# Two heads' short softmax rows in one buffer, turned by one transpose, in a causal attention and feed-forward kernel

## The chip, the cores and the metric

The kernel runs on one core of a Trainium2 chip, in fp32. The metric is device time in microseconds (us) of one execution. A core has five engines that run side by side, each in its own instruction order: TensorE (PE, matrix multiplies; PEld is its weight load), VectorE (DVE), ScalarE (ACT), GpSimd (POOL) and SyncE (SP, which here issues the DMA transfers). PE writes into PSUM banks; the other data lie in SBUF, 128 partitions wide.

## The reference

```python
# x: (8, 1024, 256); 16 heads of 64
def attn(x):                                    # Wq, Wk, Wv: (16, 256, 64); Wp: (1024, 256)
    idx = clip(pos[None, :] - pos[:, None] + 16, 0, 32)
    bias = transpose(rel_table[idx], (2, 0, 1))
    q, k, v = (einsum('btc,hcd->bhtd', x, W) for W in (Wq, Wk, Wv))
    scores = einsum('bhtd,bhsd->bhts', q, k) / sqrt(64) + bias[None]
    w = softmax(where(causal, scores, -inf), axis=-1)
    out = einsum('bhts,bhsd->bhtd', w, v)
    return out.transpose(0, 2, 1, 3).reshape(8, 1024, 1024) @ Wp + bp
def ffn(x):
    x_prev = x shifted by one row of T (zeros first)
    xr, xk = mu * x + (1 - mu) * x_prev         # with mu_r and mu_k
    return sigmoid(xr @ W_r.T) * (square(relu(xk @ W_k.T)) @ W_v.T)
x = x + layernorm(attn(layernorm(x)))
x = x + layernorm(ffn(layernorm(x)))
```

## The kernel before

The attention is cut into 64 units: 8 batch rows times 8 pairs of heads. The 1024 query rows of a unit are 8 blocks (`tb` 0 to 7) of 128 rows. Block `tb` needs scores against the first n = 128 (tb + 1) keys only. Blocks 4 to 7 are "long" (n over 512, done in two parts), blocks 0 to 3 are "short". A unit has four steps, each with one long and one short block (`STEPS`).

For one block, `do_scores` records these tasks. PE multiplies q and k of both heads into PSUM (line 1041; 64-row tiles, so that two heads and two halves of the rows run together; short blocks take two of the four shared `pm` banks, long blocks their own ring `sl`). DVE adds the bias near the diagonal (line 1070) and takes the negated row maximum (line 1078). ACT writes the exponentials from PSUM to an SBUF buffer `p` of one head and sums them (line 1098), which frees the bank. DVE takes the reciprocal of the sum (line 1165). POOL scales `p` in place (line 1186), one instruction for a short block of one head, two for a long one.

`turn` then has DVE transpose `p` in 32 x 32 blocks into the tile `blocks` (line 1207), one instruction for each head. `blocks` has the axes `[partition, r, slot, head, 32]`; a slot is a 32-column block of one row block. When the row blocks of a group (`GROUPS`: two groups of four row blocks in each unit) are turned, `shuffle` issues 16 DMA copies from SP (line 1267) that move 32-partition bands from `blocks` to a tile `d`, so that the blocks become full transposes. `do_av` multiplies `d` with v on PE (line 1293), and ACT saves the result (line 1316). In the last unit the second group, tb 4, 2, 5 and 3, is transposed by PE instead (`turn_by_pe`). All other matmuls (projections, the feed-forward part) go through the helper at line 433 with 128-row tiles.

Buffers come from rings: a `Ring` of n buffers gives the next owner its buffer when the users of the owner n places before are done. The ring for short `p` has four buffers of 512 columns, the one for long `p` four of 1024. In the last batch row the feed-forward part borrows such rings for its tiles (`buf` in `stages_ffn`).

The order of the work is not that of the source. `add` records a task with its engine, a guessed cost and its dependencies. `Planner.simulate` plays all tasks with these costs; each engine takes, of the tasks that are ready, the one with the lowest key, and the instructions are issued in that order. A key is the task's own priority plus `RANK` of its kind (named after its functions, so `dve:one.go` is the transpose of one head), times 9. The plan is cut into stretches of 34 us; for each, a seed in `SEEDS` draws random offsets for the ranks of all kinds, in the order of their sorted names (seed 0: none), and for the planner's reluctance to let PE pass between score tiles (64 rows) and the other matmuls (128 rows), for which it reckons 0.09 us. A prologue (the first loads and projections) is planned before, without seeds.

Of the kernel before, what the change touches and what calls it, by code (L numbers as in the profile page):

```python
# [92 lines left out]

STRETCH = 34
SEEDS = (
    392905, 816692, 244547, 283470, 560662, 39100, 216772, 294259, 588279, 412218,
    371534, 0, 431774, 883409, 180062, 984965, 373709, 0, 0, 0,
    763639, 658110, 822178, 930278, 665013, 718545, 0, 952361, 100832, 846644,
    0, 137572, 647438, 377597, 0, 469262, 83528, 641677, 323164, 611824,
    444950, 813510, 452093, 622742, 919130, 335621, 0, 751616, 573689, 0,  # L100
    0, 99909, 466380, 402426, 0, 986219, 146830, 82811, 0, 0,
    151578, 369797, 955240, 0, 0,
)


# [252 lines left out]
def tile_attn_ffn_block(  # L358
# [16 lines left out]
    nc = tc.nc  # L375
    B, T, C = x.shape
    H, _, D = Wq.shape
    P = 128
    NT = T // P
    NC = C // P  # L380
# [4 lines left out]
    CT = 2 * P  # L385
    HB = 512
    BW = P + MAX_REL
    WL = P - 1 + BW
    QD = 32
    NQ = P // QD  # L390
# [25 lines left out]
    acts = ctx.enter_context(tc.tile_pool(name="acts", bufs=1))  # L416
# [3 lines left out]
    add = plan.add  # L420
# [8 lines left out]
    def matmul(dst, lhs, rhs, first, last):  # L429
# [21 lines left out]
        "v": Ring(acts, [P, NT, P], "v", 1),  # L451
        "sl": Ring(ps_l, [P, 2, HB], "sl", 2),
        ("p", "long"): Ring(acts, [P, T], "pl", 4),
        ("p", "short"): Ring(acts, [P, HB], "ph", 4),
        "carry": Ring(small, [P, NC], "carry", 2),
    }
    for what in ("in", "ao", "y", "f"):
# [294 lines left out]
    def stages_ffn(b, c):  # L752

        box = {}

        def buf(name, tag, spare):

            if b < B - 1:
                return R[tag](f"{name}_{b}_{c}")
            return R[spare](  # L760
                f"{name}_{b}_{c}", lambda t: t[:, : NC * CT].rearrange("p (k f) -> p k f", k=NC)
            )

        def s0(prio):
            box["rn"] = norm_stats(ys[b, c], f"y_{b}_{c}", prio)

        def s1(prio):
            box["yn"] = buf("yn", "yn", ("p", "short")) if c % 2 else R["yn"](f"yn_{b}_{c}")
            normed(box["yn"], ys[b, c], box["rn"], f"y_{b}_{c}", prio, edge=b == B - 1)

        def s2(prio):
# [175 lines left out]
    NU = len(units)  # L947
# [67 lines left out]
    def do_scores(u, tb, prio):  # L1015


        n = (tb + 1) * P
        size = "long" if n > HB else "short"
        parts = [(0, n // 2), (n // 2, n)] if n > HB else [(0, n)]  # L1020
        pr = units[u][1]
        q, k = qkv[u, "q"], qkv[u, "k"]
        what = f"{u}_{tb}"
        ps = [R["p", size](f"p_{what}_{hh}") for hh in range(2)]
        nmax, tot, rcp = (R[x, size](f"{x}_{what}") for x in ("nmax", "tot", "rcp"))
        z = {"u": u, "tb": tb, "n": n, "p": ps}

        def part(i, c0, c1):

            sl = R["sl"](f"s_{what}_{i}") if size == "long" else None  # L1030
            keep = [sl] if sl else []

            def s(hh):
                return sl.tile[:, hh, : c1 - c0] if sl else pm(t, hh)[:, : c1 - c0]

            def go():
                for half in range(2):
                    for hh in range(2):
                        rows = slice(hh * D, (hh + 1) * D)
                        o = half * D  # L1040
                        nc.tensor.matmul(  # L1041
                            s(hh)[o : o + D],
                            q.tile[rows, tb * P + o : tb * P + o + D],
                            k.tile[rows, c0:c1],
                            start=True,
                            stop=True,
                        )

            t = add(
                "pe",  # L1050
                0.05 + (c1 - c0) * 0.00169,
                go,
                r=[(q, tb // 4)] + [(k, g) for g in range((c1 - 1) // HB + 1)],
                w=keep,
                prio=prio,
                mode="rows",
                banks=0 if sl else 2,
            )
            z.setdefault("scores", t)
            w = min(n, BW)  # L1060
            ready = {hh: t for hh in range(2)}

            def bias(h0, h1):
                def go():
                    if sl:
                        dst = sl.tile[:, :, c1 - c0 - w : c1 - c0]
                        src = bm[:, 2 * pr : 2 * pr + 2, BW - w :]
                    else:
                        dst, src = s(h0)[:, n - w : n], bm[:, 2 * pr + h0, BW - w :]
                    nc.vector.tensor_tensor(dst, dst, src, ALU.add)  # L1070

                cost = 0.07 + (h1 - h0) * w / 960
                done = add("dve", cost, go, t, bm_done, r=keep, prio=prio - 0.5)
                ready.update({hh: done for hh in range(h0, h1)})

            def top(h0, h1):
                def go():
                    nc.vector.tensor_reduce(  # L1078
                        nmax.tile[:, i, h0:h1],
                        sl.tile[:, :, : c1 - c0] if sl else s(h0),  # L1080
                        AX.X,
                        ALU.max,
                        negate=True,
                    )

                return add(
                    "dve",
                    0.075 + (h1 - h0) * (c1 - c0) / 960,
                    go,
                    ready[h0],  # L1090
                    r=keep,
                    w=[(nmax, i)],
                    prio=prio - 0.5,
                )

            def exp(hh, max_done):
                def go():
                    nc.scalar.activation(  # L1098
                        ps[hh].tile[:, c0:c1],
                        s(hh),  # L1100
                        AF.Exp,
                        bias=nmax.tile[:, i, hh : hh + 1],
                        scale=1.0,
                        accum_out=tot.tile[:, i, hh : hh + 1],
                    )

                add(
                    "act",
                    0.26 + (c1 - c0) * 0.00083,
                    go,  # L1110
                    max_done,
                    r=keep,
                    w=[ps[hh], tot],
                    prio=prio - 0.1,
                    frees=None if sl else (t, hh),
                )

            if sl:
                if c1 == n:
                    bias(0, 2)  # L1120
                done = top(0, 2)
                for hh in range(2):
                    exp(hh, done)
            else:
                for hh in range(2):
                    bias(hh, hh + 1)
                    exp(hh, top(hh, hh + 1))
# [7 lines left out]
        if size == "long":  # L1135
            total = R["part", size](f"part_{what}")

            def behind():
# [10 lines left out]
                r=[rcp],  # L1149
                w=[rcp],  # L1150
                prio=prio - 0.1,
# [14 lines left out]
            r=[total],  # L1166
            w=[inv],
            prio=prio - 0.6,
        )
        if size == "long":  # L1170
# [6 lines left out]
                r=[inv, rcp],  # L1177
                w=[rcp],
# [3 lines left out]
        def scale(hh):  # L1182
            def go():
                for i, (c0, c1) in enumerate(parts):
                    p = ps[hh].tile[:, c0:c1]
                    nc.gpsimd.tensor_scalar(  # L1186
                        p, p, rcp.tile[:, i, hh : hh + 1], 1.0, ALU.mult, ALU.mult
                    )

            cost = 0.25 * len(parts) + n / 1220  # L1190
            add("pool", cost, go, r=[ps[hh], rcp], w=[ps[hh]], prio=prio)

        for hh in range(2):
            scale(hh)
# [2 lines left out]
    def turn(z, prio):  # L1197

        tb, n, u = z["tb"], z["n"], z["u"]
        k = tb // 2  # L1200
        g = 0 if k in GROUPS[0] else 1
        s0 = GROUPS[g][k] + 1 - tb % 2
        state = blk.setdefault(g, {"turns": [], "move": []})

        def one(hh, p):
            def go():
                nc.vector.transpose(  # L1207
                    blocks[g][:, :, s0 : s0 + 2 * tb + 1 : 2, hh, :].rearrange(
                        "p r a j -> p a r j"
                    ),  # L1210
                    p.tile[:, :n].rearrange("p (a r j) -> p a r j", r=NQ, j=QD),
                )

            state["turns"].append(
                add("dve", 0.065 + n / 960, go, *state["move"], r=[p], prio=prio)
            )

        for hh in range(2):
            one(hh, z["p"][hh])

    def turn_by_pe(z, g, prio):

        tb, u = z["tb"], z["u"]
        s0 = GROUPS[g][tb // 2] + 1 - tb % 2
        if (u, g) not in dd:
            dd[u, g] = R["d"](f"d_{u}_{g}")
# [2 lines left out]
        def some(hh, a0, a1):  # L1229
            def go():  # L1230
                for a in range(a0, a1):
                    matmul(
                        pm(t)[:, (a - a0) * P : (a - a0 + 1) * P],
                        z["p"][hh].tile[:, a * P : (a + 1) * P],
                        ident,
                        True,
                        True,
                    )

            t = add("pe", 0.217 * (a1 - a0), go, r=[z["p"][hh]], prio=prio, banks=1)  # L1240

            def place():
                n = a1 - a0
# [311 lines left out]
```

## Time and profile before

| | |
|---|---|
| median of 3 runs | 2194.66 us (2192.37 to 3990.92) |
| profiled execution, its own time | 2193.71 us |
| its span in the profile | 2191.9 us |
| granted TensorE clock, mean | 0.998 |
| busy PE, PEld | 2161.1 us (99%), 1182.6 us (54%) |
| busy DVE, ACT, POOL | 1970.5 us (90%), 1377.4 us (63%), 1526.8 us (70%) |
| transposes at line 1207 | 1016, 724.2 us |
| POOL scales at line 1186 | 1536, 883.9 us |

An engine's busy time is the time in which it has an instruction at work. Rows of groups read "line, engine, operation, output <- inputs, shapes, count | total busy us, mean ns of one | idle us of the engine just before them, and what ended it". In PE's timeline a row merges equal matmuls that follow each other; one fp32 matmul of the source leaves two records there, so `x8` of 512 columns is four matmuls. Ends of matmuls are modelled and overlap the next start; starts are not. A row of stretches gives the stretch, its length, then busy time and count for PE, PEld, DVE, ACT and POOL, the granted PE clock, the DMA engines' busy share and GB/s.

### The profile page before, as it was taken

To read this page: it belongs to the slowest core of one execution; us is meant where nothing else is said; L and a number is where in the kernel's file an instruction comes from. 1 tells how busy PE (TensorE), PEld (TensorE's weight loads), DVE (VectorE), ACT (ScalarE), POOL (GpSimd) and SP (SyncE) were. 2 spreads that over 40 slices of the span, in tenths; PEclk is the share of its full clock that TensorE was granted. 3 is DMA by queue.
4 is the path that set the end of the run, shared out by engine and by line. 5 is a ranking of instruction groups with operands and counts; after the bars stand their busy time and mean duration, and the time that the engine had idled before them with its cause. 6 is when DMAs were issued, how large, how long until landed. Compare 5 with 4: busy or idle time off the path is not lost.

```text
span 2191.9 us, 61295 instructions
## 1 busy us (share of the span) xinstructions
PE 2161.1 (99%) x21312; PEld 1182.6 (54%) x21312; DVE 1970.5 (90%) x4460; ACT 1377.4 (63%) x4314; POOL 1526.8 (70%) x3709
## 2 busy tenths in 40 slices
PE   7999999999999999999999999999999999999997
PEld 3455555555555555555555555555555555555565
DVE  5998999999998999998999989899889998999776
ACT  5665756666566565665656666565666756667454
POOL 4666677766786768775687766777667775687553
PEclk9999999999999999999999999999999999999999
DMA  5887877867778687776877777777787868877560
GB/s 166 193 199 184 194 175 179 202 167 181 178 179 200 166 193 177 183 189 169 196 180 188 181 189 181 170 175 192 170 190 178 198 167 198 193 177 189 131 152 25
DMA packets 272596, 388.92 MB, mean 177 GB/s; under 512 B 142624, under 2 KB 199968, under 8 KB 272160
## 3 DMA queue, kind: packets, MB, share of 16 engines
q1 hardware_dynamic: 272144, 384.87, 73.3%
q8 instruction: 170, 2.79, 0.6%
q14 instruction: 138, 1.13, 0.2%
q10 hardware_dynamic: 144, 0.14, 0.0%
HBM read 59.91 MB, written 25.29 MB: 39 GB/s over the span
## 4 chain that ended last, share of the span: by engine, by line
PE 89%; DVE 5%; DMA 1%; POOL 1%; issue 1%; ACT 1%; SPq 1%; ACTq 0%; DVEq 0%; POOLq 0%
PE pm L433 46%; PE pm L1293 21%; PE s L1041 16%; PE pm L1041 6%; DVE blocks L1207 2%; DVE nmax L1078 2%; POOL p L1186 1%; SPq L1267 1%; ACT p L1098 0%; DMA d<-blocks 0%; DVE pm L1070 0%; DMA out_dram<-r 0%; DVE s L1070 0%; DMA tab<-in_L_attn_rel_table_dram 0%; DVE y L722 0%
## 5 line engine op out<-in xcount | busy, mean ns | idle before, releaser
L1186 POOL TENSOR_SCALAR p<-p,rcp 128x512 f32<-128x512 f32 (+5 forms) x1536 | 883.9, 595 | 86.0 <-DVE rcp L1165 62.7
L1098 ACT ACTIVATE p<-s,nmax 128x512 f32<-128x512 f32 (+3 forms) x1024 | 616.0, 607 | 398.4 <-DVE nmax L1078 317.4
L1207 DVE STREAM_TRANSPOSE blocks<-p 128x256 f32<-128x256 f32 (+2 forms) x1016 | 724.2, 749 | 50.6 <-POOL p L1186 41.6
L1078 DVE TENSOR_REDUCE nmax<-s 128x2 f32<-128x1024 f32 (+3 forms) x512 | 516.7, 1009 | 33.3 <-PE s L1041 30.1
L1293 PE MATMUL pm<-d,v 128*64 128x256 f32 (+1 forms) x5120 | 523.5, 359 | 0.3 <-DMA d<-blocks 0.3
L1293 PEld LDWEIGHTS pm<-d,v 128*64 128x64 f32 x5120 | 351.8, 137 | 219.4 <-issue 39.6
L1041 PE MATMUL s<-k,q 64*64 64x512 f32 (+3 forms) x4096 | 444.3, 519 | 5.9 <-ACT p L1098 5.7
L1098 ACT ACTIVATE p<-pm,nmax 128x256 f32<-128x256 f32 (+3 forms) x512 | 270.9, 531 | 94.5 <-DVE nmax L1078 68.9
L433 PEld LDWEIGHTS pm<-wv,xnT 128*64 128x64 f32 x4096 | 226.5, 137 | 52.0 <-issue 26.9
L433 PE MATMUL pm<-wv,xnT 128*64 128x128 f32 x4096 | 248.1, 274 | 0.0
L433 PE MATMUL pm<-xnT,wk 128*64 128x512 f32 x1024 | 245.5, 600 | 0.1
L1078 DVE TENSOR_REDUCE nmax<-pm 128x1 f32<-128x256 f32 (+3 forms) x512 | 242.1, 478 | 3.4
L433 PE MATMUL pm<-xnT,wq 128*64 128x512 f32 x1024 | 244.7, 599 | 0.0
L433 PE MATMUL pm<-wp_sb,oT 128*64 128x256 f32 x2048 | 240.5, 381 | 0.7 <-ACT oT L1316 0.7
L1041 PEld LDWEIGHTS s<-k,q 64*64 64x64 f32 x4096 | 133.6, 132 | 180.2 <-issue 95.2
L1098 ACT ACTIVATION_READ_ACCUMULATOR p<-s,nmax 128x1 f32 x1024 | 206.7, 202 | 0.0
L433 PEld LDWEIGHTS pm<-wp_sb,oT 128*64 128x64 f32 x2048 | 141.6, 137 | 101.7 <-issue 25.2
L1041 PE MATMUL pm<-k,q 64*64 64x256 f32 (+3 forms) x2048 | 188.4, 438 | 0.0
L1070 DVE TENSOR_TENSOR pm<-pm,bm 128x144 f32<-128x144 f32 (+1 forms) x512 | 135.3, 298 | 38.1 <-PE pm L1041 36.9
L1140 POOL TENSOR_TENSOR rcp<-nmax 128x2 f32<-128x2 f32 x256 | 51.0, 199 | 148.5 <-DVE nmax L1078 119.0
L1155 POOL TENSOR_TENSOR tot<-tot,rcp 128x4 f32<-128x4 f32 x256 | 52.1, 203 | 146.8 <-ACT rcp L1148 139.8
L433 PEld LDWEIGHTS pm<-xnT,wq 128*64 128x64 f32 x1024 | 68.0, 137 | 129.7 <-issue 104.4
(103 smaller groups left out, 2266.2 us busy)
## 6 DMA issues: line engine op xcount, KB each, us to landing
d<-blocks SPq DMA_DIRECT2D x2032, 144.0 KB, 2.6
xin<-in_L_attn_x_dram SPq DMA_DIRECT2D x32, 256.0 KB, 3.0
wq<-in_L_attn_Wq_dram SPq DMA_DIRECT2D x128, 64.0 KB, 2.2
wk<-in_L_attn_Wk_dram SPq DMA_DIRECT2D x128, 64.0 KB, 2.2
wv<-in_L_attn_Wv_dram SPq DMA_DIRECT2D x64, 128.0 KB, 2.9
xre<-in_L_attn_x_dram SPq DMA_DIRECT2D x32, 256.0 KB, 3.0
out_dram<-r SPq DMA_DIRECT2D x32, 256.0 KB, 2.2
via_in<-st_in SPq DMA_DIRECT2D x112, 64.0 KB, 1.9
```

The costliest lines, as they stand in the source:

```text
L433: nc.tensor.matmul(dst[rows], lhs[:, rows], rhs, start=first, stop=last)
L1041: nc.tensor.matmul(s(hh)[o : o + D], q.tile[rows, tb * P + o : tb * P + o + D], k.tile[rows, c0:c1], start=True, stop=True,)
L1070: nc.vector.tensor_tensor(dst, dst, src, ALU.add)
L1078: nc.vector.tensor_reduce(nmax.tile[:, i, h0:h1], sl.tile[:, :, : c1 - c0] if sl else s(h0), AX.X, ALU.max, negate=True,)
L1098: nc.scalar.activation(ps[hh].tile[:, c0:c1], s(hh), AF.Exp, bias=nmax.tile[:, i, hh : hh + 1], scale=1.0, accum_out=tot.tile[:, i, hh : h ...
L1140: nc.gpsimd.tensor_tensor(rcp.tile[:, 0, :], m1, m0, ALU.subtract)
L1155: nc.gpsimd.tensor_tensor(tot.tile, tot.tile, rcp.tile, ALU.mult)
L1186: nc.gpsimd.tensor_scalar(p, p, rcp.tile[:, i, hh : hh + 1], 1.0, ALU.mult, ALU.mult)
L1207: nc.vector.transpose(blocks[g][:, :, s0 : s0 + 2 * tb + 1 : 2, hh, :].rearrange("p r a j -> p a r j"), p.tile[:, :n].rearrange("p (a r j) ...
L1267: nc.sync.dma_start(d.tile[r * QD : (r + 1) * QD, q].rearrange("p s h j -> p (s h j)"), blocks[g][q * QD : (q + 1) * QD, r].rearrange("p s ...
L1293: nc.tensor.matmul(dst, v[:, jt, rows], src, start=(jt == 0), stop=(jt == 2 * k + 1),)
```

## The change

For short blocks, both heads' exponentials now go into one buffer of 1024 columns. They lie in turn by blocks of 32 columns: 32 of head 0, 32 of head 1, and so on. `p_of` gives the view of one head, which ACT writes and POOL scales. One DVE transpose (`both` in `turn`) then reads the 2n columns and writes both heads' slots, whose 32 columns lie side by side in `blocks`. In the last unit, tb 2 and 3 go to `turn_by_pe`; there the heads lie one after the other. The ring for short `p` becomes two buffers of 1024 columns. In the last batch row the feed-forward tile `yn` of c = 1 moves to the ring of v and that of c = 3 to the ring of long `p`. `dve:both.go` has no entry in `RANK` (the transpose of one head, `dve:one.go`, has 1.8). All 65 seeds are replaced. The built program has 254 DVE instructions fewer; PE, ACT, POOL and SP have as many as before, in another order.

```diff
 SEEDS = (
-    392905, 816692, 244547, 283470, 560662, 39100, 216772, 294259, 588279, 412218,
...
+    424466, 663855, 192028, 0, 417825, 336004, 961170, 927691, 447616, 808813,
...
-        ("p", "short"): Ring(acts, [P, HB], "ph", 4),
+        ("p", "short"): Ring(acts, [P, 2 * HB], "ph", 2),
...
-            box["yn"] = buf("yn", "yn", ("p", "short")) if c % 2 else R["yn"](f"yn_{b}_{c}")
+            box["yn"] = buf("yn", "yn", "v" if c == 1 else ("p", "long")) if c % 2 else R["yn"](f"yn_{b}_{c}")
...
-        ps = [R["p", size](f"p_{what}_{hh}") for hh in range(2)]
+        if size == "long":
+            ps = [R["p", size](f"p_{what}_{hh}") for hh in range(2)]
+        else:
+            ps = [R["p", size](f"p_{what}")] * 2
+        mixed = size == "short" and (u < NU - 1 or tb < 2)
...
+        def p_of(hh, c0, c1):
+            if size == "long":
+                return ps[hh].tile[:, c0:c1]
+            if not mixed:
+                return ps[hh].tile[:, hh * n : (hh + 1) * n]
+            return ps[hh].tile[:, : 2 * n].rearrange("p (b h j) -> p b h j", h=2, j=QD)[:, :, hh, :]
...
                     nc.scalar.activation(
-                        ps[hh].tile[:, c0:c1],
-                        s(hh),
+                        p_of(hh, c0, c1),
+                        same(s(hh)),
                         AF.Exp,
...
-                    w=[ps[hh], tot],
+                    w=[(ps[hh], hh), tot],
...
-                    p = ps[hh].tile[:, c0:c1]
+                    p = p_of(hh, c0, c1)
                     nc.gpsimd.tensor_scalar(
...
-            add("pool", cost, go, r=[ps[hh], rcp], w=[ps[hh]], prio=prio)
+            add("pool", cost, go, r=[(ps[hh], hh), rcp], w=[(ps[hh], hh)], prio=prio)
...
+        def both(p):
+            def go():
+                nc.vector.transpose(
+                    blocks[g][:, :, s0 : s0 + 2 * tb + 1 : 2, :, :].rearrange(
+                        "p r a h j -> p a r (h j)"
+                    ),
+                    p.tile[:, : 2 * n].rearrange("p (a r j) -> p a r j", r=NQ, j=2 * QD),
+                )
+
+            state["turns"].append(
+                add("dve", 0.065 + 2 * n / 960, go, *state["move"], r=[p], prio=prio)
+            )
...
+        if z["p"][0] is z["p"][1]:
+            return both(z["p"][0])
         for hh in range(2):
             one(hh, z["p"][hh])
```

## The prediction

> **What bounds the kernel now.** I read the page first, for engine shares and the chain; then the stretches of the span; then PE's timeline, start to start; then the groups by shape for prices; last, the waits and the landing of the shuffles.
>
> ```profile
> PE 2161.1 (99%) x21312; PEld 1182.6 (54%) x21312; DVE 1970.5 (90%) x4460; ACT 1377.4 (63%) x4314; POOL 1526.8 (70%) x3709
> PE 89%; DVE 5%; DMA 1%; POOL 1%; issue 1%; ACT 1%; SPq 1%; ACTq 0%; DVEq 0%; POOLq 0%
> ```
>
> PE is busy 99% of the 2191.9 us and holds 89% of the chain that ended last; DVE comes second. The stretches (length, then busy time of PE, PEld, DVE, ACT, POOL) show where PE is not fed:
>
> ```profile
> 0.00:100.00 100.00, 86.22 (x778) 41.64 (x778) 72.77 (x165) 62.74 (x185) 54.19 (x143) 0.98 0.69 179
> ...
> 500.00:1000.00 500.00, 499.98 (x4934) 272.85 (x4932) 460.37 (x1048) 320.22 (x1010) 365.99 (x882) 1.00 0.77 183
> 1000.00:1500.00 500.00, 498.07 (x4901) 270.82 (x4898) 463.31 (x1042) 321.19 (x1017) 363.51 (x881) 1.00 0.76 181
> 1500.00:2140.00 640.00, 639.99 (x6404) 356.13 (x6402) 568.78 (x1275) 396.44 (x1248) 443.13 (x1078) 1.00 0.74 177
> 2140.00:2192.00 52.00, 39.25 (x412) 27.28 (x408) 35.86 (x115) 25.29 (x51) 19.23 (x38) 0.93 0.08 26
> ```
>
> Only the first 100 us and the last 52 us have holes. Since busy PE is not PE at its peak, I went to PE's timeline and took starts of successive groups:
>
> ```profile
> 2069.46 0.66 PE L1041 MATMUL pm<-k,q 64*64 64x256 f32 x8
> 2069.95 1.90 PE L1041 MATMUL s<-k,q 64*64 64x512 f32 x16
> 2071.77 1.95 PE L433 MATMUL pm<-wp_sb,oT 128*64 128x256 f32 x16
> 2073.55 1.89 PE L433 MATMUL pm<-xnT,wk 128*64 128x512 f32 x8
> 2075.27 1.92 PE L433 MATMUL pm<-wv,xnT 128*64 128x128 f32 x32
> 2077.11 0.45 PE L1041 MATMUL pm<-k,q 64*64 64x128 f32 x8
> ```
>
> The eight 512-column records at 2073.55 are followed 1.72 us later. The closest such pair (108.13 and 109.84 us) is 1.71 apart. I set the price at 1.707 us for 4096 columns on the 128-row array (two records at a time) and for 8192 columns of the 64-row score matmuls (four at a time); what is too little in it shows up in the borders below. By that price all matmuls need 2037.8 us. What exceeds it lies at borders between groups. From 100 to 2140 us the medians are 0.056 us from score group to score group (380 borders), 0.015 us from 128-row group to 128-row group (768), but 0.110 us into scores (272) and 0.115 us out of them (273): 2075.27 to 2077.11 is 1.84, not 1.72. The whole span is 8.4 before the first matmul + 2037.8 + 136.2 at borders + 9.5 after the last matmul. Of the 136.2, only 24.4 us lie in gaps over 0.35 us, which are true stalls: 12.3 before 100 us, 6.3 (eight places) from 100 to 2140 us, 5.8 after. So even a kernel without one stall would take 2167.5 us, 1.1% less.
>
> **The change, part by part.**
>
> *Transposes.* For each row block tb of 0 to 3, two DVE transposes become one of twice the width. Both sizes have rows:
>
> ```profile
> L1207 DVE STREAM_TRANSPOSE blocks<-p 128x1024 f32<-128x1024 f32 x128 | 153.8, 1219 | 6.4 <-POOL p L1186 5.7
> ...
> L1207 DVE STREAM_TRANSPOSE blocks<-p 128x768 f32<-128x768 f32 x126 | 116.0, 944 | 5.5 <-POOL p L1186 4.4 <-DMA via_in<-st_in 0.7
> ...
> L1207 DVE STREAM_TRANSPOSE blocks<-p 128x512 f32<-128x512 f32 x126 | 83.0, 686 | 7.4 <-POOL p L1186 5.6 <-DMA d<-blocks 1.1 <-DMA wk<-in_L_attn_Wk_dram 0.2
> ...
> L1207 DVE STREAM_TRANSPOSE blocks<-p 128x384 f32<-128x384 f32 x126 | 66.4, 552 | 7.1 <-POOL p L1186 7.1
> ...
> L1207 DVE STREAM_TRANSPOSE blocks<-p 128x256 f32<-128x256 f32 x128 | 50.4, 422 | 10.4 <-POOL p L1186 5.2 <-DMA d<-blocks 3.4 <-POOL part L1156 1.1
> ...
> L1207 DVE STREAM_TRANSPOSE blocks<-p 128x128 f32<-128x128 f32 x128 | 31.8, 281 | 2.2 <-POOL p L1186 2.1
> ```
>
> Saved per pair: 2 x 281 - 422 = 140 ns, 2 x 422 - 686 = 158, 2 x 552 - 944 = 160, 2 x 686 - 1219 = 153. Times 64, 64, 63 and 63 pairs (the last unit turns tb 2 and 3 on PE): 9.0 + 10.1 + 10.1 + 9.6 = 38.8 us of DVE in 254 instructions fewer. DVE goes to about 1932 us (88%). None of it is on the path in the steady part: DVE's 10% idle is already there and PE's holes there sum to 6.3 us. Those eight holes stand mostly behind ACT's exponentials, which wait for DVE's maxima; I book -2 us, bounds 0 and -6.3.
>
> *The wait that is added.* A merged transpose waits for both heads' POOL scales, so the pair lands later by the merged duration less one short one: 141, 264, 392, 533 ns, 333 on average. Behind it on DVE stand the next bias adds and maxima, for which ACT's exponentials wait. What follows the transposes are SP's 16 shuffle copies (L1267, issued over about 10 us, landing 2.6 us later), then the value matmuls at L1293. From the last landing to the first such matmul the median slack is 12.2 us over 127 shuffles, the 10% point 4.0, the 5% point 2.0, the least 0.46. A delay of 0.53 us is late in one or two cases: 0 to 1 us, taken as 0.5. Without that cover it would be 127 x 0.53 = 67 us. SP's own copies are the same in number.
>
> *Buffers.* Four buffers of 512 columns become two of 1024: still two row blocks deep. In the tail, xr moves onto this ring of two, and yn of c = 1 and 3 onto v and the long ring. The built order shows the third xr behind the PE group that reads the first, ten PE groups ahead of its own use: hidden, 0.
>
> *Exponentials and scales in runs of 32 columns.* ACT has a row in 32-column runs: the 256-column oT copy takes 377 ns, and two ordinary 512-column rows, 590 ns for v and 600 for q, with the 0.83 ns a column between the exponentials of 320 and 512 columns (528 to 687), come down to 377 to 388 at 256. So 0 for ACT. POOL has no row with runs. Its 512 short scales take 46.4 + 62.5 + 128 x 0.601 + 128 x 0.700 = 275 us now. Lower bound 0 (ACT's case); upper bound 83% more, as the slowest 512-column POOL row (1281 ns at L571) stands to 700 ns: +228 us, POOL at 80%, each scale 0.45 us later. Even then POOL is not the bound, but shuffles with under 2 us of slack (6 of 127) and some exponentials come late: about +10 us at most. I take 0, the scale being, like ACT's copy, one stream in and one out, where the L571 row reads two. [...]
>
> *New seeds.* They redraw the order of all work after the prologue. In the built order PE crosses between score and 128-row groups 610 times, 570 before: 20 more each way. Each pair replaces one border of 0.056 and one of 0.015 by 0.110 + 0.115: 20 x 0.154 = +3.1 us (40 full borders would be 4.5). This is on the path, since PE has no slack. [...]
>
> **Sum.** The profiled execution took 2193.7 us (span 2191.9 and 1.8 around it). 2193.7 + 3.1 (crossings) - 2 (stalls) + 0.5 (later landings) = 2195.3; the shown median lies 1 us above the profiled time. I forecast 2195 us: no change. About 2% is what a measurement of this kernel can tell from no change. Own range: down by the other 4.3 us of steady stalls and the 4.9 us of stalls between 60 and 100 us, to about 2184; up by 1.4 (full crossings), POOL's 10 and the start's stalls drawn once more (4.9), to about 2212.
>
> **Rivals.**
>
> *A relieved DVE feeds PE everywhere* (5%). All stalls after 60 us go, tail included: 2193.7 - 4.9 - 6.3 - 5.8 + 3.1 = 2180. For it: exponentials wait 386 us for maxima. Against: those waits do not reach PE now. Even this is only 0.6% faster; over 2% (under 2150.8) would need matmul work to vanish, and not one matmul is removed, so 1% for that.
>
> *The short ring stalls PE* (5%). A merged transpose frees both heads' buffer 0.333 us later on average; the new kind of task also has no entry in the planner's rank list, where the single transpose had 1.8. If the next short exponential then waits, it keeps two of the four pm banks and PE stands. All 256 pairs at 0.333 us: 85 us, 2193.7 + 85 + 3 = 2282. It decides the verdict from 41 us on (2238 is 2%), that is 124 pairs passing their wait to PE. For it: banks and ring are shared and POOL's order changes. Against: exponentials wait for these transposes three times now, 3.2 us in all.
>
> *It does not do what it says* (3%): runs of 64 columns slow the merged transpose until it costs its two halves. DVE keeps 1970 us, and 2193.7 + 3.1 + 0.5 = 2197 follows.
>
> The forecast itself has 86%; the last 1% is over 2% faster. The rivals at 2180 and 2197 and all of the forecast lie within 2%; the ring rival is shared, four of its five parts above 2% and one below; mishaps of the new order add a little to the slow side: faster 0.01, same 0.94, slower 0.05.
>
> **What would show it.** Right: one merged row per width at 422, 686, 944 and 1219 ns, DVE near 1932 us, PE still 98 to 99%, 610 crossings at 0.11 us, scales in runs at 375 to 700 ns. Wrong: new waits of PE on p or on ACT's exponentials, of ACT on the transposes, scale rows far over 700 ns, or more than 20 us of PE gaps over 0.35 us between 100 and 2140 us.

## The result, and the profile after

The changed kernel takes 2199.82 us (median of 11 runs, 2198.43 to 2201.55), the kernel before 2193.29 us (11 runs, one of them far off at 3990.92 us, the others 2191.45 to 2195.83). The ratio is 1.0031, 95% interval 1.0023 to 1.004: 6.5 us slower, within the 2% and inside the stated range, but clear of noise, and 5 us above the forecast. The profiled execution took 2199.11 us, its span is 2197.3 us, 5.4 us longer than before.

The page of the changed kernel, shares of the engines and the chain that ended last:

```profile
PE 2166.3 (99%) x21312; PEld 1179.6 (54%) x21312; DVE 1955.4 (89%) x4206; ACT 1382.0 (63%) x4314; POOL 1518.2 (69%) x3709
...
PE 93%; DVE 3%; DMA 1%; SPq 1%; ACT 1%; POOL 0%; issue 0%; ACTq 0%; POOLq 0%; DVEq 0%
```

DVE lost its 254 instructions and 15.1 us. PE has the same 21312 records but is busy 5.2 us longer, and holds still more of the chain. The same stretches as before (length, then busy PE, PEld, DVE, ACT, POOL):

```profile
0.00:100.00 100.00, 85.77 (x772) 40.98 (x774) 75.06 (x160) 63.31 (x187) 56.18 (x147) 0.98 0.68 177
...
500.00:1000.00 500.00, 497.59 (x4868) 268.77 (x4868) 453.67 (x976) 316.39 (x994) 360.79 (x872) 1.00 0.76 181
1000.00:1500.00 500.00, 499.81 (x4920) 269.93 (x4916) 456.53 (x977) 320.56 (x1013) 359.14 (x878) 1.00 0.76 182
1500.00:2140.00 640.00, 640.00 (x6372) 354.89 (x6366) 565.63 (x1205) 397.19 (x1249) 440.98 (x1074) 1.00 0.74 177
```

PE is filled as before, but does less in the same time: from 1500 to 2140 us it is busy to the last, with 6372 records (of mixed sizes) where the kernel before had 6404. Records of mixed sizes prove little, but the count of gaps below shows that the time was lost between groups, not in holes.

The groups by shape show the merged transposes (total busy us, mean ns of one, idle of DVE before them):

```profile
L1228 DVE STREAM_TRANSPOSE blocks<-p 128x1024 f32<-128x1024 f32 x63 | 77.9, 1237 | 8.5 <-POOL p L1207 5.8 <-DMA wk<-in_L_attn_Wk_dram 2.2
...
L1228 DVE STREAM_TRANSPOSE blocks<-p 128x768 f32<-128x768 f32 x63 | 60.9, 967 | 8.7 <-POOL p L1207 8.5
...
L1228 DVE STREAM_TRANSPOSE blocks<-p 128x512 f32<-128x512 f32 x64 | 44.8, 700 | 5.1 <-POOL p L1207 2.9 <-DMA d<-blocks 1.0 <-POOL tot L1176 0.2
...
L1228 DVE STREAM_TRANSPOSE blocks<-p 128x256 f32<-128x256 f32 x64 | 27.5, 429 | 3.0 <-POOL p L1207 2.6
```

They last 7 to 23 ns longer than the rows that priced them, so runs of 64 columns cost next to nothing. Runs of 32 on POOL and ACT cost nothing. Here are the smallest two scales (line 1207) and the largest short exponential (line 1119, from `pm`):

```profile
L1119 ACT ACTIVATE p<-pm,nmax 128x512 f32<-128x512 f32 x128 | 88.2, 690 | 47.5 <-DVE nmax L1099 31.6 <-DVE part L1186 9.6 <-PE s L1062 3.7
...
L1207 POOL TENSOR_SCALAR p<-p,rcp 128x256 f32<-128x256 f32 x128 | 61.3, 486 | 34.4 <-DVE rcp L1186 29.2 <-DVE part L1186 5.1
...
L1207 POOL TENSOR_SCALAR p<-p,rcp 128x128 f32<-128x128 f32 x128 | 46.5, 375 | 19.1 <-DVE rcp L1186 17.5 <-DVE part L1186 1.4
```

Before, the exponential took 690 ns and the scales 498 and 375.

Where the 5.4 us went can be counted in PE's timeline as the prediction did: start to start of groups, less 0.2133 us (1.707 / 8) for each 512-column record with 128 rows and half of that for one with 64 rows. All kernels below have the same 2037.8 us of matmuls. Gaps over 0.35 us are called stalls and kept apart; times are of each profiled execution. Such a gap holds whatever makes a group late: a wait, but also matmuls that themselves ran slowly.

| kernel | crossings | at crossings, us | at other borders, us | stalls, us | span, us |
|---|---|---|---|---|---|
| before | 570 | 70.8 | 41.1 | 24.3 | 2191.9 |
| after | 610 | 75.9 | 41.8 | 24.3 | 2197.3 |
| e1: after, transposes parted | 610 | 76.1 | 42.0 | 25.4 | 2198.6 |
| e2: before's order, merged | 570 | 71.3 | 42.0 | 24.8 | 2193.7 |
| e3: before, 44 crossings more | 614 | 79.0 | 40.7 | 20.1 | 2195.5 |
| e4: before, 108 crossings more | 678 | 89.5 | 40.9 | 24.9 | 2211.0 |
| e5: after, other seeds | 574 | 71.8 | 42.7 | 20.6 | 2191.1 |
| e6: after, 18 crossings fewer | 592 | 72.1 | 42.7 | 40.1 | 2210.1 |
| e7: after, old seeds | 674 | 87.4 | 37.8 | 131.0 | 2312.3 |
| e8: before, new seeds | 692 | 90.3 | 37.6 | 126.8 | 2310.3 |

From before to after, crossings grew by 5.1 us (0.13 for each of 40), other borders by 0.7, stalls not at all; 0.4 us less lies at the two ends. The theory to test (A) is that the new order costs the time, and the merge nothing. Its rivals: the merge costs (B); the merge gains, and the order ate it (C).

### The profile page after: what moved, and what is told of

It reads as the page before. It is cut to its first block, busy times and chain, and to the rows that moved or that the text cites. A ratio compares the mean times of both kernels' runs of the same rounds, so it can differ in the third digit from the quotient of the medians.

```text
span 2197.3 us, 61041 instructions
## 1 busy us (share of the span) xinstructions
PE 2166.3 (99%) x21312; PEld 1179.6 (54%) x21312; DVE 1955.4 (89%) x4206; ACT 1382.0 (63%) x4314; POOL 1518.2 (69%) x3709
## 4 chain that ended last, share of the span: by engine, by line
PE 93%; DVE 3%; DMA 1%; SPq 1%; ACT 1%; POOL 0%; issue 0%; ACTq 0%; POOLq 0%; DVEq 0%
PE pm L433 47%; PE pm L1329 22%; PE s L1062 17%; PE pm L1062 7%; SPq L1303 1%; DVE nmax L1099 1%; DVE blocks L1241 1%; ACT p L1119 0%; DMA skew<-line 0%; DMA raw<-in_L_ffn_W_r_dram 0%; POOL p L1207 0%; DMA tab<-in_L_attn_rel_table_dram 0%; DVE blocks L1228 0%; DVE s L1091 0%; DVE st_f L523 0%
## 5 line engine op out<-in xcount | busy, mean ns | idle before, releaser
L1207 POOL TENSOR_SCALAR p<-p,rcp 128x512 f32<-128x512 f32 (+5 forms) x1536 | 878.9, 589 | 104.9 <-DVE rcp L1186 76.1
L1241 DVE STREAM_TRANSPOSE blocks<-p 128x1024 f32<-128x1024 f32 x508 | 510.3, 1026 | 22.4 <-POOL p L1207 20.4
L1062 PE MATMUL s<-k,q 64*64 64x512 f32 (+3 forms) x4096 | 438.1, 519 | 4.1 <-ACT p L1119 2.0
L1228 DVE STREAM_TRANSPOSE blocks<-p 128x512 f32<-128x512 f32 x254 | 211.1, 831 | 25.2 <-POOL p L1207 19.8
L1352 ACT COPY oT<-pm 128x256 f32<-128x256 f32 x256 | 89.3, 374 | 100.0 <-PE pm L1329 99.4
```

Of the source, the lines that this page charges most:

```text
L1062: nc.tensor.matmul(s(hh)[o : o + D], q.tile[rows, tb * P + o : tb * P + o + D], k.tile[rows, c0:c1], start=True, stop=True,)
L1207: nc.gpsimd.tensor_scalar(p, p, rcp.tile[:, i, hh : hh + 1], 1.0, ALU.mult, ALU.mult)
L1228: nc.vector.transpose(blocks[g][:, :, s0 : s0 + 2 * tb + 1 : 2, :, :].rearrange("p r a h j -> p a r (h j)"), p.tile[:, : 2 * n].rearrange( ...
L1241: nc.vector.transpose(blocks[g][:, :, s0 : s0 + 2 * tb + 1 : 2, hh, :].rearrange("p r a j -> p a r j"), p.tile[:, :n].rearrange("p (a r j) ...
L1352: lambda: nc.scalar.copy(o.tile.rearrange("p (t q j) -> p t q j", t=2, j=QD), pm(t, i)[:, :CT].rearrange("p (q t j) -> p t q j", t=2, j=QD),),
```

## The experiments

**e1: the new order without the merge.** `both` issues two transposes.

```diff
-                nc.vector.transpose(blocks[g][:, :, s0 : s0 + 2 * tb + 1 : 2, :, :]..., p.tile[:, : 2 * n]...)
+                for hh in range(2):
+                    nc.vector.transpose(
+                        blocks[g][:, :, s0 : s0 + 2 * tb + 1 : 2, hh, :].rearrange("p r a j -> p a r j"),
+                        p.tile[:, : 2 * n].rearrange("p (a r h j) -> p a r h j", r=NQ, h=2, j=QD)[:, :, :, hh, :],
+                    )
```

> The changed kernel with its own order, buffers and seeds, but each merged transpose (254) given as two transposes of one head, back to back at the same place of DVE's order. Theory A (the 6 us lost come from the order that the new seeds draw, above all its 40 more crossings of PE between score and 128-row groups; the merge itself is off the path): DVE's busy time goes up by about 20 us, from 1955 to about 1975, and the time stays at 2200, within 1 us. Rival B (the merge itself costs, since both heads' columns land later or the one transpose holds DVE longer): the time falls towards the kernel before, 2194 to 2197. Rival C (DVE's saved time is worth something on the path, and the order has eaten it): the time rises, to 2203 to 2206.

Measured: 2199.71 us, 1.0032 (1.0019 to 1.0044) of the kernel before, where the changed kernel has 1.0031. DVE on its page:

```profile
PE 2167.2 (99%) x21312; PEld 1180.8 (54%) x21312; DVE 1966.1 (89%) x4460; ACT 1380.7 (63%) x4314; POOL 1518.3 (69%) x3709
```

DVE has its 254 instructions back and 10.7 us more to do (20 were expected), and the time did not move. So neither B nor C: with the order held, the merge is off the path, as far as intervals of some 0.1% can tell.

**e2: the merge without the new order.** The kernel before, seeds and order of all engines kept, with the change's buffers and views; the merged transpose stands at the second one's place.

```diff
+                if b.ring.tag == "ph":
+                    b.tile = self.short(b)   # one buffer of 1024 columns for both heads, two in turn
...
         def one(hh, p):
             def go():
+                if n <= HB:
+                    begun.append(hh)
+                    if len(begun) == 2:
+                        nc.vector.transpose(...)   # both heads, as in the change
+                    return
```

> The kernel before with its own order on every engine, seeds included, but with the change's buffers, runs of 32 columns and merged transposes, each merged one standing where the second of the two stood. Crossings of PE stay at 570. Theory A: 2193.3, within 1.5 us of the kernel before, with about 20 us less busy DVE. Rival B: 2197 to 2200, since what the merge costs is all here. Rival C: under 2191, since DVE's saving is here without the new order.

Measured: 2193.61 us, 1.0007 (0.9999 to 1.0016), DVE 1954.3 us. As A has it: 16 us of DVE work taken away, and the path did not notice. With e1 this settles the question of the merge from both sides; a cost of more than 0.16% (3.5 us) is excluded here.

**e3 and e4: crossings alone.** The kernel before; in the finished plan, neighbouring groups on PE change places where this parts two groups of one mode on either side, and where the second was ready over 1 us early by the plan. 22 such exchanges (every fifth that offers itself) or 54 (every second).

```diff
         order, held, state = best
+        if rank:
+            order, _ = reorder(order, held, True, 5, 1.0)   # e4: every 2nd
```

> The kernel before, in which 22 pairs of neighbouring groups in PE's order (one score group, one 128-row group, the second ready over 1 us early by the plan) change places, so that PE crosses 614 times, 44 more than before; nothing else changes. Theory A at the price the two profiles show (5.1 us more at crossings for 40 more, 0.127 each): 2193.3 + 5.6 = 2198.9. At the net price of the prediction (0.077 each): 2196.7. Rivals B and C, in which crossings are not what costs: within 1 us of 2193.3.

> As the one with 44 more crossings, with 54 such pairs: 678 crossings, 108 more than before. Theory A at 0.127 each: 2193.3 + 13.7 = 2207; at the net price of 0.077: 2201.6. Rivals B and C: within 2 us of 2193.3. Time per crossing should agree with the run of 44 within 0.03 us.

Measured: 2198.35 us with 44 more, 1.0026 (1.0016 to 1.0035); 2213.93 us with 108 more, 1.0096 (1.0081 to 1.0111). The kernel before took 2192.47 on that chip, so these are +5.9 and +21.5 us. Crossings do cost, and 44 of them cost almost what the change lost with 40. The first hit A's number; the second came out 7 us above it, and 0.134 and 0.199 us a crossing do not agree within the 0.03 that I had asked for. The table says why: at the crossings themselves the two agree (8.2 / 44 = 0.186 and 18.7 / 108 = 0.173), but e3's stalls happen to be 4.2 us shorter and e4's 0.6 longer. The price of a crossing is thus 0.13 (the change) to 0.19 us, and the prediction's net 0.077 is refuted.

The timelines also show why an added crossing is dearer than the average one. Call the groups between two crossings a stretch, and leave out gaps over 0.35 us. Equal groups in a row count as one, as in a timeline. These are means in us, with the number of gaps:

| kernel | crossing behind a stretch of several groups | crossing behind a group that stands alone |
|---|---|---|
| before | 0.119 (497) | 0.173 (71) |
| after | 0.117 (493) | 0.171 (108) |
| e3 | 0.119 (491) | 0.174 (121) |
| e4 | 0.119 (487) | 0.171 (186) |

In a longer stretch the difference does not vanish, it shows one border later. In the kernel before, the first border behind a crossing takes 0.056 us for score groups and 0.076 for 128-row groups, and the borders after it 0.006 and 0.013. So a crossing costs 0.12 us at once and 0.05 to 0.06 behind the first group of the new mode, about 0.17 together. The crossings added in e3, in e4 and by the change are all of the kind behind a lone group. The 0.13 of the change divides by all 40, of which about seven lie in gaps counted as stalls.

**e5: the change with other seeds.** Seeds searched anew, with the planner's price of a crossing at the traces' mean.

```diff
-SWITCH = 0.09
+SWITCH = 0.125
...
 SEEDS = (
-    424466, 663855, 192028, 0, 417825, 336004, 961170, 927691, 447616, 808813,
+    158648, 158493, 96673, 0, 3011, 483296, 648624, 4574, 168656, 284896,
...
```

> The changed kernel with 65 other seeds, chosen with the planner's price of a crossing set from 0.09 to 0.125 us, the mean that the traces show. Buffers, runs of 32 columns and merged transposes stay. PE's built order crosses 574 times instead of 610. Theory A (the loss is the order's crossings): 2199.8 - 36 x 0.127 = 2195.2, within 2 us, if its stalls are like those of the two kernels. Rival B (the merge or the buffers cost, whatever the order): stays at 2198 to 2201.

Measured: 2192.91 us, 0.9997 (0.9988 to 1.0006). The loss is gone with the change's buffers, runs and merged transposes all in place, which B did not allow for. It is 2.3 us less than A's 2195.2, just outside the 2 us allowed for stalls like those before. 36 crossings fewer account for 4.1 us of the 6.2 us between the spans; shorter stalls (3.7 us) give the rest, less 0.9 at other borders and 0.7 at the ends. It draws level with the kernel before and does not beat it; no version here did.

**e6: fewer crossings in the changed kernel.** The same exchange the other way: nine pairs of groups that stood in turn are brought together.

```diff
+            order, _ = reorder(order, held, False, 1, 0.0)
```

> The changed kernel with its own seeds; in PE's order 9 neighbouring pairs of groups change places so that groups of one mode come together (only where the second was ready by the plan before the first began). 592 crossings, 18 fewer. Theory A at 0.127 each: 2199.8 - 2.3 = 2197.5; at the 0.134 of the run with 44 more: 2197.4; if an exchanged group is not ready on the chip, up to 1 us of stall each. Rival B: 2199.8, or a little more.

Measured: 2209.36 us, 1.0071 (1.0057 to 1.0085): 9.5 us slower than the changed kernel instead of 2.3 faster, a miss. Crossings did give back 3.8 us, but stalls grew by 15.8. The timelines of PE, DVE and ACT of this kernel around one of the nine exchanges (start, length, then idle of the engine before and what ended it; lines have moved: 1109 scores, 1146 maxima, 1166 exponentials, 1376 value matmuls, 1399 ACT's copy of their result, 480 the helper):

```profile
353.82 1.68 PE L1376 MATMUL pm<-d,v 128*64 128x256 f32 x16
355.43 1.09 PE L1109 MATMUL s<-k,q 64*64 64x512 f32 x8
356.34 0.61 PE L1109 MATMUL pm<-k,q 64*64 64x256 f32 x8
356.77 1.04 PE L1109 MATMUL s<-k,q 64*64 64x512 f32 x8
359.95 2.94 PE L480 MATMUL pm<-xk,wkT 128*64 128x256 f32 x16 [2.14 <-ACT oT L1399]
362.67 2.64 PE L480 MATMUL pm<-wrT,xr 128*64 128x256 f32 x16
365.14 1.04 PE L480 MATMUL pm<-wv,xnT 128*64 128x128 f32 x16
```

```profile
356.59 1.23 DVE L1146 TENSOR_REDUCE nmax<-s 128x2 f32<-128x1024 f32 x1 [3.47 <-PE s L1109]
```

```profile
358.85 0.69 ACT L1166 ACTIVATE p<-s,nmax 128x512 f32<-128x512 f32 x1 [3.27 <-DVE blocks L1288]
359.44 0.19 ACT L1166 ACTIVATION_READ_ACCUMULATOR p<-s,nmax 128x1 f32 x1
359.53 0.64 ACT L1399 COPY oT<-pm 128x256 f32<-128x256 f32 x2
```

The score group of 512 columns used to stand before the value matmuls; now it comes behind them, at 355.43, and three score groups stand together. PE saves two crossings, some 0.25 us. But the orders of DVE and ACT are as before: DVE idles 3.47 us until these scores come, ACT 3.27 us before its exponential, for a transpose that stands behind the maximum on DVE, and behind this exponential stand the copies that free the PSUM banks of the value matmuls, which had ended long before. PE's next group needs such a bank and waits 2.14 us. A crossing is cheap beside a stall, and the order trades one for the other. This is one of the nine exchanges; the others are not shown.

The wait is not the whole loss. The two groups behind it take 2.72 and 2.47 us from start to start; in the changed kernel the same two take 1.78 and 1.73:

```profile
354.33 1.95 PE L433 MATMUL pm<-xk,wkT 128*64 128x256 f32 x16
356.11 1.90 PE L433 MATMUL pm<-wrT,xr 128*64 128x256 f32 x16
357.84 1.92 PE L433 MATMUL pm<-wv,xnT 128*64 128x128 f32 x32
```

The granted TensorE clock (its share of full speed, the third number from the end) differs with them: 0.74 behind the wait in e6, 1.00 in the changed kernel.

```profile
359.00:365.50 6.50, 5.55 (x40) 3.52 (x42) 6.50 (x15) 3.14 (x10) 4.04 (x10) 0.74 0.33 67
```

```profile
350.00:365.00 15.00, 15.00 (x160) 8.89 (x158) 13.54 (x32) 9.41 (x28) 12.88 (x30) 1.00 0.76 178
```

Of the 12.8 us between the two spans, PE is idle for 7.6 (38.6 against 31.0) and busy for the other 5.2, although it crosses less.

**e7 and e8: each kernel with the other's seeds.** 

```diff
 SEEDS = (
-    424466, 663855, 192028, 0, 417825, 336004, 961170, 927691, 447616, 808813,
+    392905, 816692, 244547, 283470, 560662, 39100, 216772, 294259, 588279, 412218,
...
```

e8 has the same lines the other way round.

> The changed kernel with the old seeds. The kinds of tasks have changed, so the same seeds draw other offsets and the order is another one: 674 crossings, 64 more than in the changed kernel. Theory A: at least 2199.8 + 64 x 0.127 = 2208, and more if PE stalls in an order that nobody chose, up to 2260. Rival B says nothing of it. Rival D (any seeds do, the plan is robust): 2195 to 2202.

> The kernel before with the new seeds, the mirror of the last one: 692 crossings, 122 more than before. Theory A: at least 2193.3 + 122 x 0.127 = 2208.8, and more with stalls, up to 2260. Rival D: 2190 to 2197.

Measured: 2321.38 us, 1.0584 (1.0557 to 1.0611), and 2312.38 us, 1.0542 (1.0527 to 1.0556). Both are beyond my upper bound of 2260. Between the profiles of the changed kernel and e7 lie 115.0 us, of which 106.7 are gaps counted as stalls (131.0 - 24.3) and 11.5 crossings, less 4.0 at other borders. Not all of the 106.7 is waiting: PE is idle for 103.0 us in e7 and 31.0 in the changed kernel, 72 more. The mean granted clock is 0.986 against 0.998; over the spans that would be an estimated 28 us more of lost clock, most of the other 34.7. PE's waits in e7 (us in total, times, longest), matmuls alone:

```profile
PE s L1062 <- ACT p L1119: 52.8, 36, 6.1
PE pm L433 <- ACT p L1119: 14.0, 9, 3.9
```

Score groups wait for exponentials to free their PSUM. So seeds belong to one list of tasks: the merge brings a new kind of task into the sorted names, every later draw falls on another kind, and an order that fitted is gone.

**e9 and e10: the merge undone, once where PE stalls and once where it does not.** e7 and e5 with the edit of e1.

> The changed kernel with the old seeds, whose order stalls PE for some 115 us behind late exponentials, and with each merged transpose given as two: 15 to 20 us more busy DVE in the same order (674 crossings). Theory A1 (DVE's saved time is hidden even where PE does wait, since DVE idles 16% there): 2321, within 4 us. Theory A2 (where PE waits on exponentials that wait on DVE's maxima, DVE's time is on the path): 2328 to 2341, that is 7 to 20 us more.

> The changed kernel with the other seeds (574 crossings, 2192.9 us), each merged transpose given as two. Theory A: 2193, within 1.5 us, since nothing of DVE's time is on the path there. Rival C (the saved time is what brings it back to the level of the kernel before): 2196 to 2200.

Measured: e9 2314.22 us, 1.0554 (1.0529 to 1.058), against 1.0584 (1.0557 to 1.0611) for e7; e10 2192.68 us, 1.0004 (0.9994 to 1.0014), against 0.9997 for e5. DVE is busy 14 us longer in each (1967.1 against 1952.7, 1965.8 against 1951.3). That made neither slower. e9 came out 7 us lower, outside the 4 that I allowed, with intervals that overlap. The runs of both vary with their granted clock, and at the same clock they lie closer: 2314.1 and 2312.3 us at 0.986, 2326.7 and 2320.5 at 0.981 (e7, e9). What is sure is that e9 is not 7 to 20 us higher. Even where PE is idle for over 100 us, most of it behind exponentials, these 14 us of DVE are not what it waits for.

## Why the prediction was right, and where it was not

*The bound* held. PE is busy 98 to 99% in every kernel near 2200 us, and the forecast of no change at 2% stands. A difference far below 2% can be told here, though: the interval of the result is 0.1% to either side. The lower end of the stated range was added up wrongly: 2195.3 - 4.3 - 4.9 is 2186, not 2184; nothing hangs on it.

*Transposes.* Off the path, as said (e1, e2, e9, e10). The size was wrong: 38.8 us were booked, and line 1207's 231.6 us for short blocks became 211.1, 20.5 less (the long ones grew by 5.9, so that all of DVE shows 15.1). The step that failed is "2 x 281 - 422": it took the mean length of a record for the time that it holds the engine. The row it came from shows the difference: 128 records of 281 ns are 36.0 us, but its busy time is 31.8, since records of neighbours overlap. In the trace before, two 128-column transposes in a row start 225 ns apart and two of 256 columns 359; a pair then saves 2 x 225 - 359 = 91 ns, and 93, 108 and 96 for the wider ones (starts of 492, 625, 876 and 1154 ns): 24.6 us in all. The merged records are 7 to 23 ns longer than those rows, which takes 4 us of it back.

*The added wait* cost nothing. From the last landing of a shuffle to its first value matmul the median slack is 12.0 us after, 12.2 before, and PE shows no matmul waiting for `d`; 0.5 us had been booked. *Buffers, runs of 32 on ACT and POOL:* 0 booked, 0 found; POOL's upper bound of +228 us is empty.

*Crossings* are the mis-sized term that matters: +3.1 booked, +5.8 found with the other borders. Two choices made it small. It used the median crossing (0.110 and 0.115), where the mean without stalls is 0.125 (70.8 us over the 565 that are not stalls), and the crossings that e3 and e4 added cost 0.17 to 0.19. And it credited each pair of crossings with two borders saved, 20 x 0.071 = 1.4 us; the saved ones cost next to nothing, since from before to after the other borders fell from 1197 to 1119 while their sum rose from 41.1 to 41.8. The 0.056 taken for a border between score groups is the second part of a crossing's own cost, which each added crossing brings along; borders that can be saved cost 0.006 and 0.013. The upper bound, 4.5 for full crossings, was too low for the same reason.

*Stalls.* -2 booked for a relieved DVE; they stayed at 24.3 (12.0 before 100 us, 4.9 up to 2140, 7.4 after, against 12.3, 6.3 and 5.8). The tail's growth is one gap of PE before the first `xk`, 4.5 us instead of 2.5. That the stalls came out level was not foreseen by the mechanism but taken for granted: it belongs to these seeds, and with seeds that do not fit (e7) the same kernel takes 2321 us, far outside the stated range. With -2, +0.5 and -1.4 gone and 40 crossings at 0.127, the prediction's own sum gives 2193.7 + 5.1 = 2198.8, beside 2199.11 measured; the price is taken from that same execution, so this closes the account and does not test it.

*Rivals.* The short ring did not stall PE: PE's matmuls wait 3.2 us on exponentials, where it was 5.7. One sign of being wrong did show, ACT waiting on transposes: 13.7 us (18 times) instead of 3.2 (three times). All of it is on the long ones, e1 has as much (13.8), and PE's waits on exponentials did not grow with it. A relieved DVE did not feed PE better. The merged transposes do not cost their two halves: DVE has 1955 us, not 1970.

## What to carry to other kernels

Work taken off an engine that is 90% busy was worth nothing here, while another was 99% busy and hardly waited for it; look first at what the edit does to the order on the full engine, which the built program shows before anything runs. When an order comes from a seeded plan, seeds are part of the kernel: change one task and they must be found anew, and the difference between two seed lists can hide or feign an effect of the edit, so try the edit in the old order as well. Price an instruction by the starts of neighbours, not by its record's length, and a class of gaps by its mean, not its median, together with what it leaves behind at the next border.

## What was not expected of the hardware

DVE's records overlap: of two 128-column transposes in a row the first lasts 296 ns, yet the second starts after 225. PE's passage between 64-row and 128-row tiles costs 0.11 us at the median and 0.125 on average at the crossing itself; over 570 crossings that is 71 us, 3% of this kernel. Another 0.05 to 0.06 us fall behind the first group of the new mode, so that a crossing costs 0.17 to 0.18 in all, beside the 0.186 (e3) and 0.173 (e4) at the added ones. What PE does in these two parts was not found. Behind one of PE's waits the granted clock was lower too: a wait of 2.14 us in e6 was followed by a clock of 0.74 and by two groups that took 1.7 us more than in the changed kernel, where it was 1.00. Behind a wait of 2.08 us in e7, 1032 us into its span, it was not: over the next 10 us the clock was 1.00. What decides it was not found.
